# A two-FFN attention block on one core: rows turned on VectorE and by plain transfers, the shift's parts on ScalarE and GpSimd, all of x loaded early

## The chip, the cores and the metric

The kernel runs on one core of one Trainium2 chip. The metric is the device time of one execution, in microseconds. A core has a matrix engine (TensorE; PE in the profile, its weight loads PEld), three engines for elementwise work (VectorE = DVE, ScalarE = ACT, GpSimd = POOL), and queues that issue transfers (SyncE = SP, and the ACT queue).

## The reference, cut to what matters

The input x holds 32 sequences of 256 rows with 128 columns. Every row passes through three residual steps, and the weights of the two FFNs are signs (+1 or -1):

```python
x = x + 0.5 * ffn(layernorm(x))
x = x + attn(layernorm(x))           # attn ends in layernorm(ctx + its input) * gamma + beta
x = x + 0.5 * ffn(layernorm(x))

def ffn(x):                          # 128 -> 512 -> 512 -> 128
    h = concatenate([x, -x])         # (k0 has 256 rows)
    h = relu(s0 * h @ sign(k0)) * 2
    h = relu(s1 * h @ sign(k1)) * 2
    return s2 * h @ sign(k2)

def attn(x):                         # 16 heads of 8 columns, 256 keys
    Q, K, V = x @ Wq.T + bq, x @ Wk.T + bk, x @ Wv.T + bv
    p = softmax(Q @ K.T / sqrt(8))
    return layernorm(p @ V + x) * gamma + beta
```

## The kernel before, in words

**Units.** The work is cut into 16 units of two sequences (512 rows, four tiles of 128). A unit passes through `first` (FFN 0), `norm_attn`, `project`, then for each of its two sequences `maxima`, `shift`, `weigh`, `context`, and at last `second` (FFN 1), which stores the unit. The last unit does FFN 1 in two halves.

**Two halves of a number.** Each fp32 operand of a dense product is split into two fp16 parts, high and low, and both are multiplied. `relu_split` makes them: ACT writes the high part (L625) and DVE the low part (L626); for some tiles ACT writes the whole fp32 value instead (L628, tile `full`) and POOL subtracts (L623).

**Turning.** A dense product needs its rows turned, features on partitions. `normalize` makes the layer-normed rows: `bn_stats` on DVE (L557, L558), the power on POOL (L559, L561), then two POOL passes (L571, L572), or DVE scalings (L566) where `quick` is set. `turned` then turns them. If `quick`, PE transposes them (L585), ACT and DVE split (L588, L589). Else ACT writes the high part (L593), POOL the low part (L594), and one transposing transfer from the SP queue turns both (L595). There are 43 of these transfers: 14 for FFN 0 (`xT`), 15 for attention (`xTa`), 14 for FFN 1 (`xT_None`).

**Attention.** `project` makes Q and K on PE, splits them (L728, L730), writes them to DRAM (L733, tile `dr`) and reads them back into the layout of the score products (L738). The last rows of a Q tile hold the negated row maxima, so that the product subtracts them: the tile is first zeroed by a transfer from a zero block (L717), and the maxima come later. `maxima` makes eight score tiles `nat` per sequence (PE L781) and DVE reduces each to its negated row maxima `nm` (L792). `shift` turns the maxima into the two fp16 parts `mt`: L802 the high part, L803 the low part, both on DVE; PE transposes them (L809, tile `pm`), ACT copies (L814), and two small transfers put them into Q (L815, L816). `weigh` makes the shifted scores `sc` (PE L849), ACT takes the exponential (L861), PE multiplies with V (L831, tile `cx`). `context` transposes back (L875), divides, adds, normalizes and adds to x.

**The order.** It isn't left to the compiler. Each operation is a node with an engine, an estimated cost, a rank and what it reads and writes. `_Plan.simulate` plays the five engines forward with these costs and delays (for a transfer, a `lag` from issue to landing), and picks on each engine the lowest rank that is ready. The instruction order per engine that comes out is written down and fixed; at run time each engine runs its list in order and waits on semaphores. So an estimate that is too low in the list of costs becomes a wait on the chip. A unit of rank (`UNIT`, 16) is one unit of work; the score tiles of one sequence (`nat`) and of the sequence before it (`sc`) are issued as pairs of the same rank and use two PSUM buffers. `choose` orders PE, `relief` decides where L628 takes the place of L626. Constants at the top (`B0`, `BA`, `BP`, `B1`, `AHEAD`, `FAR` and so on) set the ranks of the stages.

The lines that matter below are these:

```python
        op(DVE, 0.2, lambda: nc.vector.tensor_scalar(mt.t[:, :, :, 0, :], nm.t, 1.0 / ONE, ...       # L802
        op(DVE, 0.12, lambda: nc.vector.scalar_tensor_tensor(mt.t[:, :, :, 1, :], nm.t, 1.0 / ONE,   # L803
            mt.t[:, :, :, 0, :], ALU.mult, ALU.subtract), r=[*nmr, (mt, 0)], w=[(mt, 1)], rank=rank)
        op(PE, 0.12, turn, r=[(mt, 0), (mt, 1), "ident16"], w=[pm], rank=(u + 0.5 * b) * UNIT + 8.06, kind="C")
```

## Time and profile before

| what | value |
|---|---|
| median of 3 runs | 693.76 us (691.03 to 695.23) |
| profiled execution | 695.02 us, of which the span is 693.2 us |
| PE busy | 644.7 us (93%) |
| DVE busy | 600.2 us (87%) |
| ACT busy | 536.6 us (77%) |
| POOL busy | 458.8 us (66%) |
| transfers | 46.69 MB, mean 67 GB/s |
| granted PE clock, mean | 0.990 |

The span runs from the first to the last instruction; the 1.8 us around it belong to the execution's own time. Busy time is a union: matmuls on different 32-column tiles of the array overlap and count once. A line such as `L809 <- DVE mt L803` names an instruction that waited and the instruction that released it.

### The profile page before, as it was taken

How to read it: one execution, taken by the hardware profiler on the slowest of the kernel's cores; microseconds unless marked ns; L12 is line 12 of the kernel's file. 1: busy time of each engine (PE TensorE's matmuls, PEld its weight loads, DVE VectorE, ACT ScalarE, POOL GpSimd, SP SyncE). 2: the span in 40 equal slices, each digit the busy share in tenths (PEclk: the TensorE clock that was granted, in tenths of full speed). 3: DMA queues.
4: the chain of work that ended last, by engine and by line, in shares of the span. 5: the costliest groups of instructions: out<-in, count | busy, mean ns of one | idle time of the engine just before them, and what ended most of it. 6: DMA issues, size and time to landing. Idle time of an engine off the chain costs nothing.

```text
span 693.2 us, 29847 instructions
## 1 busy us (share of the span) xinstructions
PE 644.7 (93%) x13082; PEld 330.4 (48%) x13082; DVE 600.2 (87%) x1227; ACT 536.6 (77%) x792; POOL 458.8 (66%) x585
## 2 busy tenths in 40 slices
PE   3989879899999999999999999999999998988997
PEld 1544434545455454545445454544545453543445
DVE  6879988889989888999988898999989888888675
ACT  3545867888889787988888788887878887877773
POOL 6766677679595958869594978866474967653110
PEclk9999979999999999999999999999999999999999
DMA  5142342323333141313323143322213151302000
GB/s 155 45 110 64 73 126 19 103 50 97 56 64 98 26 133 35 111 44 72 94 42 113 34 112 43 70 71 59 75 20 117 22 115 24 88 26 35 5 17 31
DMA packets 79398, 46.69 MB, mean 67 GB/s; under 512 B 50562, under 2 KB 74628, under 8 KB 79268
## 3 DMA queue, kind: packets, MB, share of 16 engines
q1 hardware_dynamic: 77380, 43.93, 26.5%
q8 instruction: 102, 1.67, 1.0%
q10 hardware_dynamic: 1888, 0.85, 0.5%
q14 instruction: 28, 0.23, 0.1%
HBM read 20.25 MB, written 13.24 MB: 48 GB/s over the span
## 4 chain that ended last, share of the span: by engine, by line
PE 70%; DVE 15%; ACT 9%; issue 3%; DMA 2%; SPq 1%; ACTq 0%; POOL 0%
PE p_None L386 17%; PE cx L831 15%; PE p L386 15%; PE sc L849 7%; DVE nm L792 5%; ACT pt L861 5%; PE p L383 4%; PE nat L781 3%; PE p_None L383 2%; PE tp L875 2%; DVE mt L803 2%; PE pv L386 1%; ACT qkhl L728 1%; DVE qkhl L730 1%; PE pq L383 1%
## 5 line engine op out<-in xcount | busy, mean ns | idle before, releaser
L792 DVE TENSOR_REDUCE nm<-nat 128x4 f32<-128x1024 f32 x256 | 310.8, 1217 | 35.7 <-PE nat L781 31.5
L861 ACT ACTIVATE pt<-sc,esc 128x1024 f32<-128x1024 f32 x256 | 285.7, 1118 | 71.4 <-PE nat L781 59.2
L386 PEld LDWEIGHTS <-w 128*32 128x32 f16 x4048 | 103.5, 96 | 97.6 <-issue 31.0
L831 PE MATMUL cx<-pt,vaug 128*32 128x256 f32 x2048 | 139.0, 389 | 0.0
L849 PE MATMUL sc<-Q,ks 32*128 32x256 f16 x1024 | 105.1, 275 | 12.6 <-ACT pt L861 12.2
L781 PE MATMUL nat<-ks,Q 32*128 32x256 f16 x1024 | 102.0, 274 | 2.6 <-ACT pt L861 1.3
L386 PE MATMUL p<-h1h,w 128*32 128x512 f16 x860 | 87.0, 383 | 0.1
L386 PE MATMUL p<-h1l,w 128*32 128x512 f16 x860 | 86.3, 380 | 0.0
L386 PE MATMUL p_None<-h1h_None,w 128*32 128x512 f16 x800 | 80.6, 382 | 0.9 <-ACT full L628 0.8
L831 PEld LDWEIGHTS cx<-pt,vaug 128*32 128x32 f32 x2048 | 59.0, 110 | 47.0 <-issue 16.7
L386 PE MATMUL p_None<-h1l_None,w 128*32 128x512 f16 x800 | 80.4, 379 | 0.3 <-issue 0.3
L849 PEld LDWEIGHTS <-ks 32*128 32x128 f16 x1024 | 32.9, 92 | 71.4 <-issue 65.8
L625 ACT ACTIVATE h2h<-p 128x512 f16<-128x512 f32 (+1 forms) x72 | 41.1, 572 | 22.1 <-PE p L383 11.8
L625 ACT ACTIVATE h1h<-p 128x512 f16<-128x512 f32 (+1 forms) x72 | 40.3, 575 | 14.8 <-PE p L383 10.5
L781 PEld LDWEIGHTS <-Q 32*128 32x128 f16 x1024 | 32.1, 92 | 39.1 <-issue 38.3
L626 DVE SCALAR_TENSOR_TENSOR h2l<-p,h2h 128x512 f16<-128x512 f32 (+1 forms) x63 | 41.0, 651 | 10.5 <-ACT h2h L625 10.3
L559 POOL TENSOR_SCALAR ve_a<-mv_a 128x4 f32<-128x4 f32 (+1 forms) x17 | 3.3, 194 | 69.0 <-PE sc L849 40.5
L383 PEld LDWEIGHTS <-w 128*128 128x128 f16 x308 | 29.6, 100 | 29.4 <-issue 10.5
L626 DVE SCALAR_TENSOR_TENSOR h1l<-p,h1h 128x512 f16<-128x512 f32 (+1 forms) x59 | 38.1, 655 | 4.5 <-ACT h1h L625 4.2
L625 ACT ACTIVATE h2h_None<-p_None 128x512 f16<-128x512 f32 x60 | 35.7, 595 | 6.9 <-PE p_None L386 4.2
L625 ACT ACTIVATE h1h_None<-p_None 128x512 f16<-128x512 f32 x60 | 34.5, 605 | 5.4 <-PE p_None L386 5.3
L386 PE MATMUL p_None<-xT_None,w 128*32 128x512 f16 x480 | 36.6, 390 | 0.9 <-issue 0.6
(159 smaller groups left out, 1376.5 us busy)
## 6 DMA issues: line engine op xcount, KB each, us to landing
dr<-qkhl SPq DMA_DIRECT2D x32, 256.0 KB
Q<-dr SPq DMA_DIRECT2D x48, 128.0 KB
ks<-dr SPq DMA_DIRECT2D x48, 128.0 KB
out_dram<-x SPq DMA_DIRECT2D x15, 256.0 KB
x<-in_L_attn_x_dram SPq DMA_DIRECT2D x14, 256.0 KB
Q<-nought SPq DMA_DIRECT2D x16, 128.0 KB
dm<-mr SPq DMA_DIRECT2D x32, 16.0 KB
Q<-dm SPq DMA_DIRECT2D x32, 16.0 KB
```

Of the source, the lines that this page charges most:

```text
L383: nc.tensor.matmul(to, w, of, start=start, stop=stop)
L386: nc.tensor.matmul(to[32 * r : 32 * r + 32], w[:, 32 * r : 32 * r + 32], of, start=start, stop=stop)
L625: op(ACT, 0.09 + w / 1280, lambda: nc.scalar.activation(hi.t[:, m, :], ps.t, AF.Relu), r=[ps], w=[(hi, m)], rank=rank)
L626: op(DVE, 0.08 + w / 985, lambda: nc.vector.scalar_tensor_tensor(lo.t[:, m, :], ps.t, 0.0, hi.t[:, m, :], ALU.max, ALU.subtract), r=[ps, ( ...
L728: op(ACT, 0.586, lambda i=i, pq=pq, hl=hl: nc.scalar.activation(hl.t[:, 0, :], pq.t, AF.Identity, bias=bs[:, i : i + 1]), r=[pq, "bs"], w= ...
L781: nc.tensor.matmul(nat.t[:, ii, qc, :], Q.t[32 * r : 32 * r + 32, g, b * S + qc * P : b * S + qc * P + P], K[32 * r : 32 * r + 32, g, b * ...
L792: op(DVE, 1.141, lambda g=g, pr=pr, nat=nat: nc.vector.tensor_reduce(nm.t[:, :, 2 * pr : 2 * pr + 2, g].rearrange("p q i -> p i q"), nat.t ...
L803: op(DVE, 0.12, lambda: nc.vector.scalar_tensor_tensor(mt.t[:, :, :, 1, :], nm.t, 1.0 / ONE, mt.t[:, :, :, 0, :], ALU.mult, ALU.subtract), ...
L831: nc.tensor.matmul(cx.t[32 * r : 32 * r + 32, g // 2, :], V[:, 2 * b + kc, 4 * (g // 2) + r, 16 * (g % 2) : 16 * (g % 2) + 32], pts[g, r / ...
L849: nc.tensor.matmul(sc.t[:, ii, kc, :], K[32 * r : 32 * r + 32, g, b * S + kc * P : b * S + kc * P + P], Q.t[32 * r : 32 * r + 32, g, b * S ...
L861: op(ACT, 1.012, lambda pt=pt, sc=sc: nc.scalar.activation(pt.t, sc.t, AF.Exp, scale=esc), r=[sc, "esc"], w=[pt], rank=rank - RUSH, rush=True)
L875: nc.tensor.transpose(tp.t[:, qc, 8 * c : 8 * c + 8, :].rearrange("p h n -> p (h n)"), cxT.t[:, c, bass.ts(qc, P)], ident)
```

## The change

Five things are changed together, and the ranks are set anew.

1. **Turning.** Rows that are not `quick` are turned as fp32: DVE transposes 32x32 blocks (one instruction for a unit), one plain transfer writes 256 KB to DRAM, four plain transfers of 64 KB read it back with the blocks exchanged, and only then ACT writes the high part and POOL the low part. There are 42 of these chains, and no transposing transfer is left. The two attention norms of the first two units are `quick` (one before).
2. **Shift.** The high part of the maxima is written by ACT, a scaled copy and the low part by POOL; DVE does neither.
3. **x and Q.** All units of x are loaded at the start of the SP queue. Q lives in three fixed tiles, zeroed once by POOL; a later unit zeroes only the 8 rows that the shift uses (32 KB in place of 128 KB).
4. **relu.** A new rule `divert` lets ACT write only the whole fp32 value and POOL make both halves: a cast and a subtraction.
5. **Opening.** PE runs 24 products of the identity at the start. Unit 0's norm stands ahead of the weights' preparation, the large POOL memsets wait for it, k0 is asked for earlier, two of four slices of w1 go to POOL, and two small bias transfers and their POOL copies go away.

```diff
+    if WARM:
+        warm = psum([P, P], "warm")
+        def spin():
+            for _ in range(WARM):
+                nc.tensor.matmul(warm.t, ident, ident, start=True, stop=True)
+        op(PE, 0.22 * WARM, spin, r=["ident"], w=[warm], rank=-960)
...
-            hl = buf(work, [P, 2, n, D], F16, "hl", NHL, f"hl{name}")
-            op(ACT, 0.52, lambda: nc.scalar.copy(hl.t[:, 0], xn.t), r=xns, w=[(hl, 0)], rank=rank)
-            op(POOL, 1.12, lambda: nc.gpsimd.tensor_tensor(hl.t[:, 1], xn.t, hl.t[:, 0], ALU.subtract), r=[*xns, (hl, 0)], w=[(hl, 1)], rank=rank)
-            op(SP, 1.35, lambda: nc.sync.dma_start_transpose(
-                out=xT.t.rearrange("p a (t q) -> p (a t) q", q=P), in_=hl.t.rearrange("p a t d -> p (a t d)")),
-               r=[(hl, 0), (hl, 1)], w=[(xT, i, a) for i in range(2) for a in range(0, n, 2)], rank=rank, lag=3.5)
+            tb = buf(work, [P, 4, n, 32], F32, "tb", NTB, f"tb{name}")
+            tf = buf(work, [P, 4, n, 32], F32, "tf", NTF, f"tf{name}")
+            td = buf(dram, [P, 4, n * 32], F32, "td", 4, f"td{name}")
+            op(DVE, 0.06 + n * 0.135, lambda: nc.vector.transpose(tb.t.rearrange("p j t b -> p t j b"), xn.t.rearrange("p t (j a) -> p t j a", a=32)),
+               r=xns, w=[tb], rank=rank)
+            op(SP, 0.53, lambda: nc.sync.dma_start(out=td.t, in_=tb.t.rearrange("p j t b -> p j (t b)")), r=[tb], w=[td], rank=rank, lag=1.8)
+            for j in range(4):
+                op(SP, 0.5, lambda j=j: nc.sync.dma_start(out=tf.t[32 * j : 32 * j + 32].rearrange("a i t b -> a i (t b)"),
+                                                          in_=td.t[:, j, :].rearrange("(i a) n -> a i n", i=4)),
+                   r=[td], w=[(tf, j)], rank=rank, lag=2.0)
+            tfs = [(tf, j) for j in range(4)]
+            order = lambda k: xT.t[:, k].rearrange("p (t i b) -> p i t b", i=4, b=32)
+            parts = lambda k: [(xT, k, a) for a in range(0, n, 2)]
+            op(ACT, 0.12 + 0.1 * n, lambda: nc.scalar.copy(order(0), tf.t), r=tfs, w=parts(0), rank=rank)
+            op(POOL, 0.1 + 0.255 * n, lambda: nc.gpsimd.tensor_tensor(order(1), tf.t, order(0), ALU.subtract), r=[*tfs, *parts(0)], w=parts(1), rank=rank)
...
-        e, eng, rank = (ACT, nc.scalar, -898) if u == 1 else (SP, nc.sync, (u - 2) * UNIT + B0)
+        e, eng, rank = (ACT, nc.scalar, -898) if u == 1 else (SP, nc.sync, u - (690 if u > 3 else 710))
...
-        xTs[key] = turned(xn, key[0][-1], name, n, rank, quick)
+        xTs[key] = turned(xn, key[0][-1], name, n, rank + LATE, quick)
...
+        h.pair = (l, lambda: nc.scalar.activation(full.t, ps.t, AF.Relu), full, CAST * w / 512, lambda: nc.gpsimd.tensor_copy(hi.t[:, m, :], full.t),
+                  0.1 + w / 500, low(full))
...
-        Q = buf(work, [P, G, TU], F16, "Q", 3, f"Q_{u}")
-        qs[u] = Q
-        op(SP, 0.5, lambda: nc.sync.dma_start(out=Q.t.rearrange("(x j) g n -> j x g n", j=4)[3], in_=nought), ...
+        Q = qs[j]
+        if u >= NV:
+            op(SP, 0.4, lambda: nc.sync.dma_start(out=Q.rearrange("(x j) g n -> j x g n", j=16)[3], in_=nought), ...
...
-        op(DVE, 0.2, lambda: nc.vector.tensor_scalar(mt.t[:, :, :, 0, :], nm.t, 1.0 / ONE, None, ALU.mult), r=nmr, w=[(mt, 0)], rank=rank)
-        op(DVE, 0.12, lambda: nc.vector.scalar_tensor_tensor(mt.t[:, :, :, 1, :], nm.t, 1.0 / ONE, mt.t[:, :, :, 0, :], ALU.mult, ALU.subtract),
-           r=[*nmr, (mt, 0)], w=[(mt, 1)], rank=rank)
+        op(ACT, 0.2, lambda: nc.scalar.mul(mt.t[:, :, :, 0, :], nm.t, 1.0 / ONE), r=nmr, w=[(mt, 0)], rank=rank)
+        op(POOL, 0.25, lambda: nc.gpsimd.tensor_scalar(ns.t, nm.t, 1.0 / ONE, None, ALU.mult), r=nmr, w=[ns], rank=rank)
+        op(POOL, 0.3, lambda: nc.gpsimd.tensor_tensor(mt.t[:, :, :, 1, :], ns.t, mt.t[:, :, :, 0, :], ALU.subtract), r=[ns, (mt, 0)], w=[(mt, 1)], rank=rank)
```

## The prediction

> **What bounds the kernel now.** I read the page's engine line first, then the table by stage, then the waits of PE, then the timeline around the wait that stood out. Engine line, and two rows of the table by stage (span, busy time of PE, PEld, DVE, ACT, POOL, granted clock, DMA share, GB/s):
>
> ```profile
> PE 644.7 (93%) x13082; PEld 330.4 (48%) x13082; DVE 600.2 (87%) x1227; ACT 536.6 (77%) x792; POOL 458.8 (66%) x585
> ...
> 75.30:126.30 51.00, 42.85 (x771) 20.35 (x775) 43.34 (x85) 38.08 (x50) 36.48 (x46) 0.90 0.31 65
> 126.30:541.40 415.10, 404.87 (x9060) 208.95 (x9056) 374.92 (x736) 347.28 (x507) 301.78 (x376) 1.00 0.30 72
> ```
>
> Between 126 and 541 us PE is busy 97.5%; the chain that ended last shows the same products at 199.20 and 238.33 us, so a unit takes 39.1 us there. What PE lacks is in its waits. Over the whole span:
>
> ```profile
> PEld L809 <- DVE mt L803: 18.3, 25, 1.4
> ...
> PE pm L809 <- DVE mt L803: 8.8, 14, 1.1
> ```
>
> PE's only repeated wait in the steady part is for the low half of the shift, L803. Its own row says why (duration min, median, max):
>
> ```profile
> L803 DVE SCALAR_TENSOR_TENSOR mt<-nm,mt x32: 166/898/1167, 60.6 to 647.1; 128x32 f16<-128x32 f32 x32
> ```
>
> A pass that can take 166 ns takes 898. The timeline of DVE, POOL and PE shows what it waits for:
>
> ```profile
> 205.82 1.00 DVE L803 SCALAR_TENSOR_TENSOR mt<-nm,mt 128x32 f16<-128x32 f32 x1
> 205.49 1.27 POOL L680 TENSOR_TENSOR x<-x,full 128x512 f32<-128x512 f32 x1
> 226.24 0.90 DVE L803 SCALAR_TENSOR_TENSOR mt<-nm,mt 128x32 f16<-128x32 f32 x1
> 225.93 1.16 POOL L623 TENSOR_TENSOR h2l_None<-full,h2h_None 128x512 f16<-128x512 f32 x1
> 205.87 0.28 PE L849 MATMUL sc<-Q,ks 32*128 32x256 f16 x1
> 206.87 0.23 PE L809 MATMUL pm<-ident,mt 128*32 128x128 f16 x1 [0.60 <-DVE mt L803]
> ```
>
> L803 ends at 206.82 and 227.14, the POOL pass under way at 206.76 and 227.09: it ends 0.05 us after it, both times. The kernel's list holds it for 0.12 us, so PE meets `pm` too early.
>
> **The parts, and their sum.** The sum goes against the profiled span of 693.2 us; its execution took 695.02, so 1.8 lie around it, and the median is 1.3 below that execution.
>
> *Shift: the gain.* After a pair of score tiles, PE's next work normally starts 0.33 us after the pair (203.04 to 203.37). At 205.87 it starts at 206.87: 0.67 lost. In the unit's other sequence the pair at 226.23 is followed by two pieces of 0.22 each, so `pm` was due at 226.99 and starts at 227.19: 0.20 lost. Read so at all 32 `pm`, the losses come to 14 us (ten steady units at about 0.9, and single ones of 0.7 to 1.2 at the start and the end). The 8.8 and 18.3 us of the wait rows bound it: 8.8 below, 27 above.
>
> The new chain is ACT's high part, POOL's scaled copy and POOL's difference. ACT: nearest rows L814 (32x256, 352 ns) and L404 (128x128, 0.30). POOL: L538 copies 128x32 in 237 ns; a subtraction of 128x256 takes 613. So 0.55 us at best, and at worst behind one exponential (1.12) and one 1.04 pass that the order puts between POOL's two: 3.1. The old chain took 1.6 (reduction ends 205.22, L803 206.82). The new order also gives more cover: from the last score pair to `pm` PE has one `cx` piece (1.00), 24 `pq` (1.29, the row of 24 such matmuls), a score pair (0.33) and three quarters of layer 2 (1.34), 3.96 in all, against 2.83 before (203.37 to 206.20). In the other sequence the cover grows by 0.4. With POOL's 0.24 + 1.04 + 0.3 = 1.6, as long as the old chain but with 1.1 and 0.4 more cover, the wait falls to nothing or to a tenth each: 3 us left of 14. I take -11, with 0 and -14 as ends, and the worst chain as a rival.
>
> *Turning: off the path if it lands in time.* DVE gains 42 block transposes. The trace has none; the nearest rows are a reduction of 1024 elements in 1217 ns, thus 0.6 for 512, and the 128x256 addition L895 at 510, thus 1.0. At 0.6 it is +25 us; the shift's two passes (0.270 + 0.665, 32 times) give back 30, 23 fewer L626 some 15, 11 more L678 cost 8. DVE's load falls by about 12, and PE covers it: 375 of 415 us before. ACT writes the high part as before, 0.62; it gains the shift's 10 us and loses 8 of L679. POOL gains about 43 us (20 more subtractions at 1.16, 20 casts at about 1, 32 times 0.5 for the shift; 11 fewer L680 at 1.27) and reaches 72%. SP issues 210 transfers for 43; at 0.5 to 0.6 each against 1.27 this is some 60 us more on a queue that mostly sleeps.
>
> The length of the chain counts. A plain 256 KB write landed 2.0 us after its issue at 211.51, and 3.3 when a transposing transfer was ahead (204.21). The reads: four issues at 0.6, and the last lands 2.3 to 3.2 us after it is issued (the `ks` reads at 216.18 and 45.34). Then ACT 0.62 and POOL 1.16: 2.0 + 1.8 + 2.3 + 1.8 = 7.9 us at best, 10.0 at worst. In the changed order PE has some 9.7 us of work between the transpose of FFN 1's rows and their first product, and 19 to 29 us for the other two kinds. So two chains in three are covered; FFN 1's is covered by -0.3 to +1.8. What is late there first is ACT's copy, and behind it in ACT's list stands the next exponential. I take +2 for 14 such chains, ends 0 and +15.
>
> The Trainium skill speaks against this part: "DMA: Bandwidth & Descriptors", section "Rules for kernel authors", wants turns done by the transposing transfer, since a plain copy with a rearranged pattern is put at 19 times its cost. In the trace a transposing transfer needed 2.5 us from issue to its last packet (202.88 to 205.4); by that factor each turn would need an estimated 47 us, and every unit would stand still for tens of microseconds. I go by the rows, because DVE exchanges the single elements and the transfers move runs of 512 B, and this trace has plain transfers of such runs at ordinary times.
>
> *Opening: -3.5.* The chain that ended last has, in the first layer:
>
> ```profile
> 13.30 2.29 PE p L383 x5
> ...
> 15.80 5.23 PE p L383 x18
> ...
> 24.03 0.97 PE p L383 x4
> ```
>
> That is 458, 290 and 243 ns each, and 216 from 18.5 on: PE starts at half clock. Twenty-three matmuls lose 5 x 242 + 18 x 74 ns = 2.5 us. The 24 spin products start when the identity is there, at about 1.4 us. The `cx` rows price an fp32 product of 256 columns at 0.43 us, thus 0.22 for 128, twice that at half clock. So the spin ends between 6.6 and 11.8 us and the clock is up for the first layer. The norm itself waited: L559 of unit 0 began at 5.83 behind three memsets although its statistics were there at 4.7, and the scalings L566 took 0.7 a pair (1.37 and 1.41 us rows, other work between) behind further memsets. Freed, the first product could start near 10.5 in place of 13.30. Both together give at most 5.5; since the spin may end late and x of unit 1, which DVE now needs before unit 0 is through, shares the queue with more loads, I take 3.5, ends 0 and 6.
>
> "TensorE: Matmul & The Clock Gate", section "What's actually happening", puts full clock after one busy window of about 3.4 us; here it came about 7 us after the first PE work at 11.2. By the page the spin would end near an estimated 9 us, by the trace's 7 us near 10.
>
> *The rest: 0.* Loading x at once adds 3 MB to the opening's transfers, hidden behind 40 us in which only unit 0's and 1's rows are needed. The smaller zeroing saves 1.6 MB that nothing waited for. PE has the same products, 536 changes of tile shape against 546. The end (from 626 us, PE 56.6 busy of 66.9) keeps its order; I allow 4 us either way for it and for the start of the pipeline.
>
> Sum: 693.2 - 11 + 2 - 3.5 = 680.7, with 1.8 around it 682.5 where the profiled execution has 695.02; against the median that is 681.
>
> **The rivals.** *A new wait eats the gain (685 to 700).* FFN 1's chain at its worst costs 1.1 us for 14 units, 15 us; with the shift's gain of 11 and the opening the time is 693.8 - 11 - 3.5 + 15 = 694. For: ACT and POOL run their lists in order, and 9.7 us of cover is no more than the chain. Against: before, transfers nearly as long are met by PE without a wait.
>
> *DVE becomes the bound.* Before, 375 us of DVE in 10.6 units are 35.3 a unit of 39.1; at 0.6 a transpose it becomes about 34.6 of 38.2, at 1.0 it is 35.6. Only from 2.0 us each would DVE set the pace; at 1.5 its queueing already costs PE a few tenths a pair, and the time stays near 688.
>
> *The slower side: the shift waits behind long POOL passes.* The difference now stands in POOL's list, where the passes are of 1.04 to 1.27 us, and its high half behind ACT's exponential. At the worst chain of 3.1 us, 1.5 more than the old one, the added cover of 1.1 and 0.4 is passed by 0.4 and 1.1, so PE loses 0.75 more than before at each of 32 shifts: 693.8 + 24 - 3.5 = 714. It is slower by 1% from a chain of about 2.7 us, against the 1.6 that I take. Against: POOL has 28% idle.
>
> *It does nothing:* if L803 was late only because PE was early anyway, and the next wait stands right behind, only the opening remains: 690.
>
> **How the numbers follow.** The forecast, 0.62, with its own range of 674 to 688. A new wait eats the gain 0.18, DVE 0.04, nothing 0.03, slower side 0.13. The range reaches from a full 14 + 6 with a little at the end, 670, to the upper end of the new wait and part of the slower side, 700. One per cent, about what a measurement can tell from no change here, is 6.9 us: below 686.9 lies nearly all of the forecast and some of the second case, 0.68; 0.18 within; 0.14 above 700.7.
>
> **What would show it.** Right: no wait of PE on `mt`, or a tenth each; units at 38.0 to 38.3 us in the steady part; the first layer at 216 ns a matmul, first score tile near 46 us (49.3 before). Wrong: ACT idle before the copy of FFN 1's rows for a transfer, PE waiting on `pm` for POOL, block transposes above 1.5 us, or units still near 39.

## The result and the profile after

The changed kernel is slower: a median of 711.81 us (710.64 to 714.74, four runs) against 692.39 us for the kernel before (690.72 to 695.23, four runs on the same chip). The ratio is 1.0282, with an interval of 1.023 to 1.0335. The forecast was 681, in a range of 670 to 700. The profiled execution has a span of 711.2 us against 693.2.

The engine line of the page says little: PE, DVE and ACT are busy for nearly as long as before, and POOL for 41 us more.

```profile
PE 653.0 (92%) x12862; PEld 336.0 (47%) x12862; DVE 605.4 (85%) x1199; ACT 533.1 (75%) x817; POOL 499.7 (70%) x681
```

The table by stage says where the 18.0 us are. I cut both kernels at the same events: the first score tile of unit 0, of unit 2's second sequence, and of unit 13's second sequence. The columns are the stretch, its length, busy time of PE, PEld, DVE, ACT, POOL, granted clock, DMA share and GB/s. The kernel after:

```profile
0.00:58.00 58.00, 45.23 (x260) 26.11 (x264) 40.83 (x119) 23.65 (x51) 34.90 (x56) 0.88 0.41 125
58.00:137.20 79.20, 66.04 (x1331) 31.64 (x1332) 68.64 (x125) 54.62 (x82) 58.09 (x76) 0.98 0.24 74
137.20:571.20 434.00, 422.66 (x9151) 215.08 (x9148) 392.59 (x751) 356.86 (x537) 344.11 (x456) 1.00 0.26 83
571.20:711.20 140.00, 119.07 (x2138) 63.15 (x2134) 103.34 (x206) 98.01 (x148) 62.58 (x96) 0.98 0.14 45
```

The kernel before, cut at the same events:

```profile
0.00:49.30 49.30, 36.19 (x208) 17.89 (x212) 36.29 (x124) 23.47 (x48) 33.32 (x55) 1.00 0.41 108
49.30:126.30 77.00, 67.91 (x1306) 31.70 (x1310) 68.49 (x127) 54.71 (x78) 54.14 (x63) 0.93 0.30 68
126.30:560.50 434.20, 423.97 (x9469) 218.72 (x9469) 390.27 (x760) 362.36 (x527) 317.31 (x394) 1.00 0.30 70
560.50:693.20 132.70, 116.64 (x2119) 62.07 (x2115) 105.16 (x219) 96.06 (x141) 53.99 (x75) 0.99 0.16 43
```

So the opening lost 8.7 us, the start of the pipeline 2.2, the end 7.3, and the eleven steady units, where most of the 11 us were to be gained, moved by 0.2. Yet the wait that was to go did go. These are rows of the waits after (engine, line, what was waited for: total, times, longest):

```profile
PEld L874 <- POOL mt L869: 4.7, 6, 1.2
PE pm L874 <- POOL mt L869: 2.8, 4, 1.0
PE pv L423 <- issue: 4.1, 4, 1.4
PE p L423 <- issue: 2.1, 2, 1.2
ACT xT_None L653 <- DMA tf_None<-td_None: 6.4, 4, 2.6
```

PE now waits at `pm` four times where it waited 14 times, and the pass that makes the low half has one duration, where the old one ranged up to 1167 ns (the row of L869: minimum, median, maximum):

```profile
L869 POOL TENSOR_TENSOR mt<-ns,mt x32: 247/252/258, 69.1 to 663.1; 128x32 f16<-128x32 f32 x32
```

Counted by one rule, from the score pair to `pm`, the losses at the 32 `pm` fell from 15.8 to 8.0 us, and in a steady unit from 1.02 to 0.18. (The prediction's reading gave 14 for the 15.8; this count leaves some 0.08 at a `pm` that meets no wait. PE's plain idle time in the same stretches fell from 9.6 to 3.8.) What took the place of the wait shows in the other rows of that fence. "issue" is time in which the engine waited for nothing that the profile shows. The timeline of PE has it a few microseconds behind a `pm` that met no wait:

```profile
456.14 0.22 PE L874 MATMUL pm<-ident,mt 128*32 128x128 f16 x1
...
457.24 0.85 PE L423 MATMUL pv<-wqkv,xTa 128*32 128x128 f16 x48
457.90 0.40 PE L423 MATMUL p<-xT,w 128*32 128x512 f16 x4
459.54 0.40 PE L423 MATMUL p<-xT,w 128*32 128x512 f16 x4 [1.23 <-issue]
```

PE stands still for 1.23 us in the middle of a group of equal products, with no semaphore to wait for. This happens six times after, 0.89 to 1.37 us each and 7.1 in all (6.2 of them in the steady part), and twice before, 1.6 in all. The place gives the cause away. Counted over PE's weight loads and products and the few dozen semaphore and drain instructions among them, the first instruction behind each stop is number 194 of a block of 256, in both kernels and in every experiment below that has a stop. Each time a packet of 16 KB in the DMA queue of kind "instruction" had landed 1.4 to 1.5 us before PE went on (1.1 to 1.6 over all runs). The queue's row, after (packets, MB, share):

```profile
q8 instruction: 100, 1.64, 1.0%
```

PE has 25,782 such instructions. Without the first 193 they make 99.96 blocks of 256. The kernel before has 26,228, thus 101.7 blocks, and 102 such packets; rounded up, the count gives the number of packets in every run below. So PE's program arrives in blocks of 256 instructions, and PE stops where it has run through a block before the next one is there. At the stops of all these traces the 256 before had gone by in 2.1 to 3.6 us of running; some blocks as fast don't stop, so the time alone decides nothing (256 in 2.3 us at 496 us in the kernel after). The small products on quarters of the array go by so fast (`pv`: 96 instructions in 0.67 us). The changed order sets `pv` and the quartered layer 2 close together, and the wait at `pm` no longer stands between them.

### The profile page after: what moved, and what is told of

Read it like the earlier page. It is cut to its first block, busy times and chain, and to the rows that moved or that the text cites. A ratio compares the mean times of both kernels' runs of the same rounds, so it can differ in the third digit from the quotient of the medians.

```text
span 711.2 us, 29766 instructions
## 1 busy us (share of the span) xinstructions
PE 653.0 (92%) x12862; PEld 336.0 (47%) x12862; DVE 605.4 (85%) x1199; ACT 533.1 (75%) x817; POOL 499.7 (70%) x681
## 4 chain that ended last, share of the span: by engine, by line
PE 54%; DVE 19%; DMA 9%; ACT 6%; POOL 5%; issue 3%; SPq 3%; ACTq 0%; DVEq 0%; POOLq 0%
PE p_None L423 13%; PE p L423 11%; PE cx L896 11%; DVE nm L855 9%; PE sc L914 5%; PE p L420 5%; PE p_None L420 3%; DMA tf_None<-td_None 3%; ACT pt L926 2%; PE nat L844 2%; DVE h1l_None L683 2%; SPq L647 2%; PE tp L940 1%; DMA x<-in_L_attn_x_dram 1%; DMA dr<-qkhl 1%
## 5 line engine op out<-in xcount | busy, mean ns | idle before, releaser
L914 PE MATMUL sc<-qs,ks 32*128 32x256 f16 x1024 | 106.7, 274 | 17.9 <-ACT pt L926 17.2
L844 PE MATMUL nat<-ks,qs 32*128 32x256 f16 x1024 | 101.4, 274 | 9.6 <-DVE nm L855 2.7
L423 PE MATMUL p<-h1h,w 128*32 128x512 f16 x716 | 70.8, 384 | 0.2 <-DVE qkhl L793 0.2
L423 PE MATMUL p<-h1l,w 128*32 128x512 f16 x716 | 70.5, 382 | 0.0
L844 PEld LDWEIGHTS <-qs 32*128 32x128 f16 x1024 | 32.1, 92 | 44.7 <-issue 44.2
L420 PEld LDWEIGHTS <-w 128*128 128x128 f16 x342 | 33.3, 101 | 35.6 <-issue 14.9
L683 DVE SCALAR_TENSOR_TENSOR h2l_None<-p_None,h2h_None 128x512 f16<-128x512 f32 x51 | 35.1, 688 | 16.2 <-ACT h2h_None L682 15.9
L680 POOL TENSOR_TENSOR h2l<-full,h2h 128x512 f16<-128x512 f32 (+1 forms) x32 | 36.3, 1134 | 7.6 <-ACT full L685 7.4
L680 POOL TENSOR_TENSOR h1l<-full,h1h 128x512 f16<-128x512 f32 (+1 forms) x31 | 34.0, 1098 | 9.8 <-ACT full L685 9.5
L420 PE MATMUL p<-h1h,w 128*128 128x512 f16 (+1 forms) x109 | 38.5, 365 | 1.3 <-DVE h1l L683 0.5
L420 PE MATMUL p<-h1l,w 128*128 128x512 f16 (+1 forms) x109 | 38.2, 363 | 0.0
```

Source lines behind the costliest of these rows:

```text
L420: nc.tensor.matmul(to, w, of, start=start, stop=stop)
L423: nc.tensor.matmul(to[32 * r : 32 * r + 32], w[:, 32 * r : 32 * r + 32], of, start=start, stop=stop)
L680: return lambda: nc.gpsimd.tensor_tensor(lo.t[:, m, :], of.t, hi.t[:, m, :], ALU.subtract)
L683: l = op(DVE, 0.08 + w / 985, lambda: nc.vector.scalar_tensor_tensor(lo.t[:, m, :], ps.t, 0.0, hi.t[:, m, :], ALU.max, ALU.subtract), r=[p ...
L844: nc.tensor.matmul(nat.t[:, ii, qc, :], Q[32 * r : 32 * r + 32, g, b * S + qc * P : b * S + qc * P + P], K[32 * r : 32 * r + 32, g, b * S ...
L914: nc.tensor.matmul(sc.t[:, ii, kc, :], K[32 * r : 32 * r + 32, g, b * S + kc * P : b * S + kc * P + P], Q[32 * r : 32 * r + 32, g, b * S : ...
```

## The experiments

Kernels whose names begin with b are edits of the kernel before, those with a of the kernel after. In all of them the planner's order is kept, and only what is named is changed. The table is in microseconds: the median of the runs, its ratio to the kernel before on the same chip with the interval (over the chips that kernel's median goes from 690.3 to 693.4, so small differences of medians are to be read by the ratios), and from the profiled run the first score tile, the steady part, the end (both cut as above) and PE's stops for its program.

| kernel | median | ratio, interval | first tile | steady | end | stops |
|---|---|---|---|---|---|---|
| before | 692.39 | | 49.3 | 434.2 | 132.7 | 1.6 |
| after | 711.81 | 1.0282, 1.023–1.0335 | 58.0 | 434.0 | 140.0 | 7.1 |
| b_shift | 704.34 | 1.0192, 1.0171–1.0213 | 48.3 | 443.3 | 134.3 | 2.6 |
| a_shift_back | 713.28 | 1.0326, 1.0308–1.0344 | 55.4 | 435.7 | 140.6 | 1.0 |
| a_memsets | 702.09 | 1.0163, 1.0117–1.021 | 53.0 | 434.3 | 137.9 | 7.4 |
| a_xlater | 705.59 | 1.0214, 1.0187–1.0241 | 55.6 | 432.9 | 138.2 | 5.2 |
| a_nospin | 704.10 | 1.0165, 1.0138–1.0193 | 57.0 | 429.9 | 138.1 | 4.6 |
| a_pvD | 699.84 | 1.0098, 1.0066–1.0129 | 57.8 | 427.2 | 137.3 | 2.0 |
| a_pvD_shift_back | 711.22 | 1.0257, 1.0213–1.03 | 57.5 | 433.4 | 139.6 | 0.7 |
| b_pm32 | 705.46 | 1.0191, 1.0166–1.0216 | 47.4 | 440.4 | 140.9 | 0.7 |
| b_pm32_pvD | 705.88 | 1.0186, 1.0164–1.0207 | 48.1 | 441.7 | 140.3 | 3.4 |
| a_turn_list | 727.11 | 1.0478, 1.044–1.0517 | 57.1 | 449.3 | 136.0 | 3.0 |
| a_mem_x_pvD | 695.47 | 1.0033, 1.0009–1.0058 | 50.0 | 426.2 | 136.8 | 2.9 |
| a_mem_x_pvD_l2D | 692.78 | 0.999, 0.9968–1.0012 | 50.9 | 425.7 | 135.8 | 0 |
| a_end | 712.44 | 1.0275, 1.0242–1.0308 | 57.9 | 435.8 | 138.8 | 8.1 |
| a_best | 692.40 | 0.9991, 0.9976–1.0007 | 50.0 | 425.6 | 137.0 | 0 |
| a_best2 | 698.72 | 1.0088, 1.006–1.0116 | 56.1 | 425.7 | 135.6 | 0 |

### b_shift: the engine switch alone

```diff
-        nc.vector.tensor_scalar(mt.t[:, :, :, 0, :], nm.t, 1.0 / ONE, None, ALU.mult)
-        nc.vector.scalar_tensor_tensor(mt.t[:, :, :, 1, :], nm.t, 1.0 / ONE, mt.t[:, :, :, 0, :], ALU.mult, ALU.subtract)
+        nc.scalar.mul(mt.t[:, :, :, 0, :], nm.t, 1.0 / ONE)
+        nc.gpsimd.tensor_scalar(ns.t, nm.t, 1.0 / ONE, None, ALU.mult)
+        nc.gpsimd.tensor_tensor(mt.t[:, :, :, 1, :], ns.t, mt.t[:, :, :, 0, :], ALU.subtract)
```

> The kernel before with its written-down order kept, and only the shift's parts changed: ACT writes the high part, POOL the scaled copy and the low part, each at the place where DVE had them. Theory: the shift's gain is real and stands by itself. PE's losses at pm (some 0.7 us in one sequence of a unit and 0.2 in the other) fall to a tenth each, L803's 0.9 us pass is gone, and the time falls by 8 to 12 us, to 681 to 685. Rival: the next wait stands right behind this one; the losses at pm vanish but PE waits elsewhere, and the time stays at 689 to 693.

It is 14 us slower than the kernel before, and neither side had that. The losses at `pm` rose to 27.3 us. The timeline shows the slower rival of the prediction at work, a long POOL pass ahead of the short one:

```profile
206.13 1.26 POOL L680 TENSOR_TENSOR x<-x,full 128x512 f32<-128x512 f32 x1
207.35 0.25 POOL L809 TENSOR_TENSOR mt<-ns,mt 128x32 f16<-128x32 f32 x1
207.66 0.23 PE L814 MATMUL pm<-ident,mt 128*32 128x128 f16 x1 [1.31 <-POOL mt L809]
```

The scaled copy had ended at 206.05. The difference then stood behind 1.26 us of other work. So the engine switch by itself lengthens the wait in the old order. The next run shows that the new order by itself doesn't remove it either. The two belong together: the new order puts more PE work ahead of `pm` and mostly keeps long passes out of POOL's list there.

### a_shift_back: the switch undone in the new order

```diff
-        nc.scalar.mul(mt.t[:, :, :, 0, :], nm.t, 1.0 / ONE)
-        nc.gpsimd.tensor_scalar(ns.t, nm.t, 1.0 / ONE, None, ALU.mult)
-        nc.gpsimd.tensor_tensor(mt.t[:, :, :, 1, :], ns.t, mt.t[:, :, :, 0, :], ALU.subtract)
+        nc.vector.tensor_scalar(mt.t[:, :, :, 0, :], nm.t, 1.0 / ONE, None, ALU.mult)
+        nc.vector.scalar_tensor_tensor(mt.t[:, :, :, 1, :], nm.t, 1.0 / ONE, mt.t[:, :, :, 0, :], ALU.mult, ALU.subtract)
```

> The changed kernel with its order kept, and only the shift's parts put back on DVE, at the places where ACT and POOL had them. Theory: the shift's gain is inside the 711 us and was paid away elsewhere, so taking it back costs what was forecast: low parts of about 0.9 us, PE's waits on mt return, 719 to 724 us. Rival: the changed order has enough cover before pm that it is indifferent who makes the parts: 709 to 713 us and no more than 0.1 us lost at each pm.

The wait came back and the time hardly followed it: 713.28 against 711.81, and the intervals of the two ratios overlap. Two rows of its waits:

```profile
PEld L874 <- DVE mt L869: 19.9, 18, 2.5
PE pm L874 <- DVE mt L869: 15.0, 16, 2.2
```

The losses at `pm` are 24.4 us, 16 more than after, and PE's stops for its program fell from 7.1 to 1.0. In the steady part alone PE now idles 8.7 us at `pm` in place of none, and 0.6 at stops in place of 6.2; the part is 1.7 us longer. A PE that waits at `pm` gives the next block time to arrive. There one wait stood in for another, and that suggested the next experiment. The losses at the start and the end aren't followed here; the opening was 2.6 us shorter, within the spread shown below.

### a_pvD: fewer instructions for the same products

`pv` runs on the whole array, in 24 instructions a unit in place of 96.

```diff
-  dense(pv.t[:, t, :], xT.t[:, b, bass.ts(t, P)], wqkv[:, 2, a, :], tiling, k == 0, k == 2)
+  dense(pv.t[:, t, :], xT.t[:, b, bass.ts(t, P)], wqkv[:, 2, a, :], "D", k == 0, k == 2)
```

> The changed kernel with its order kept; only the value products pv are issued as 12 products of the whole array in place of 48 of a quarter each, 24 instructions in place of 96 in each unit, for the same 0.67 us. Theory: PE's stalls without a semaphore (7.1 us in six places) come from 256 instructions going by faster than the next 16 KB of program arrive, so with 72 fewer in the densest stretch they shrink to under 3 us; two more changes of the tile shape a unit cost up to 3 us; time 706 to 710. Rival: the stalls don't hang on the number of instructions; they stay at about 7 us and the time rises by the changes of shape, to 713 to 716.

It is 12 us faster than after, more than was expected. Two stops are left, 0.64 us at the start of the end part and 1.35 in the steady part:

```profile
488.72 0.27 PE L914 MATMUL sc<-qs,ks 32*128 32x256 f16 x1 [1.35 <-issue]
```

The steady part fell by 6.8 us, where the stops fell by 4.9 (6.2 to 1.35):

```profile
134.80:562.00 427.20, 422.08 (x8757) 213.95 (x8748) 392.82 (x751) 356.97 (x537) 344.31 (x456) 1.00 0.26 84
```

The other 1.9 there aren't assigned. The rest of the 12 lies at the start and the end, where it isn't separated from the spread between runs of one opening (below).

### a_pvD_shift_back: the switch undone where the program is no limit

The edits of a_pvD and a_shift_back together.

> The changed kernel with its order kept, the value products issued as 24 instructions a unit in place of 96 (as in a_pvD, 699.8 us), and the shift's parts back on DVE (as in a_shift_back). Theory: in the changed kernel the wait at pm and the wait for the next 16 KB of program stand in the same 4 us of a unit, so that one takes the place of the other and a_shift_back cost only 1.5 us. With the program's wait gone, the shift's gain must show: 708 to 712 us, some 10 above a_pvD, and about 1.2 us lost again at one pm in each unit. Rival: PE is held to the same pace by something else in that stretch; within 3 us of a_pvD.

It takes 711.22 against 699.84: 11.4 us lost by putting the shift's two passes back on DVE (6.2 of them in the steady part), where the same edit cost 1.5 with quartered `pv`. Its row of the waits, beside stops of only 0.7:

```profile
PE pm L874 <- DVE mt L869: 15.7, 16, 2.2
```

So in the new order the switch is worth some 11 us once PE's program is out of the way. That this is the prediction's own number is partly luck. The passes stand here at places that were not made for them, and PE idles 17.8 us ahead of the `pm`, not the 9.6 of the kernel before.

### a_memsets: the nine large memsets moved on POOL

```diff
+        after(pows[0], blank[0])
+        after(next(t for t in pows if t[1] == "a"), blank[1] + take(("ones", 1)))
+        after([g[0].tag for g in order if g[0].tag and g[0].tag[0] == "mult"][1], blank[2] + take(("ones", 2)))
```

Each set of three moves to another place of POOL's list: the first behind the powers of unit 0's norm, the second behind those of the first attention norm, the third behind a later norm.

> The changed kernel with its order kept, but POOL's nine large memsets moved: those of the first tile set into the time in which POOL idles (6.6 to 12.4 us), the others behind 37 us. Theory: the opening lost its time because DVE's scalings L612 of unit 1 (5.65 us for four that need 1.0) and L543 (2.45 us against 0.2) stood still beside POOL's memsets. Then L612 ends near 19 us in place of 22.1, L543 takes 1.2 us or less, the first score tile starts at 53 to 55 us in place of 58.0, and the time is 706 to 709. Rival: the opening is late because of x and PE's order; first score tile at 57 to 58 and 710 to 712 us.

The theory of the opening holds: the first score tile comes at 53.0 in place of 58.0. The kernel takes 702.09 (two runs, 704.39 and 699.79), faster than was expected; what the start and the end gave isn't explained. Behind this stands a lock between DVE and POOL. In the kernel after, DVE's four scalings of unit 1 lie beside an unbroken row of POOL work, and one instruction on 3x3 elements beside another row, which lasts from 31.77 to 34.14 (timeline of DVE, POOL and PE):

```profile
16.43 5.75 DVE L612 TENSOR_SCALAR fxn<-x,mv_f,rs_f 128x128 f32<-128x128 f32 x4
31.71 2.45 DVE L543 TENSOR_SCALAR diag<-ident,top 3x3 f32<-3x3 f32 x1
...
16.67 2.26 POOL L680 TENSOR_TENSOR h1l<-full,h1h 128x512 f16<-128x512 f32 x2 [0.30 <-ACT full L685]
18.87 1.39 POOL L576 MEMSET vaug<- 128x1536 f32 x1
20.19 0.96 POOL L577 MEMSET ks<- 128x1024 int32 x1
21.08 0.95 POOL L584 MEMSET qs<- 128x1024 f32 x1
...
22.17 0.69 PE L632 MATMUL t<-ident,fxn 128*128 128x128 f32 x2 [2.65 <-DVE fxn L612]
```

The scalings end at 22.18 and the POOL row at 22.03. With the memsets elsewhere, the same instructions in a_memsets take half of that, and a tenth for the small one:

```profile
17.48 2.85 DVE L630 TENSOR_SCALAR fxn<-x,mv_f,rs_f 128x128 f32<-128x128 f32 x4
...
28.42 0.21 DVE L561 TENSOR_SCALAR diag<-ident,top 3x3 f32<-3x3 f32 x1
```

The two differences, 2.9 and 2.2, come to the 5.0 us by which the first score tile came earlier.

### a_xlater: most of x behind the weights

```diff
+        after("wide", take("x"))
```

Fourteen loads of x move behind the loads of the projections on the SP queue.

> The changed kernel with its order kept, but the 14 loads of x for units 2 to 15 moved behind the loads of the projections on the SP queue (about 21 us in place of 2 and 11 us). Theory: x of unit 1 landed 6.9 us after its issue because the 512 KB of units 2 and 3 went ahead of it, and DVE, which wants it before it goes on with unit 0, waited until 10.35 us. Then it lands near 8 us, the scale inputs with it, the first product starts at 11 us or earlier in place of 12.72, and the first score tile 1 to 2 us earlier than 58.0. Rival: the load is late behind k1 on its own queue; it lands at 10 us as before, nothing in the opening moves, and the time stays at 710 to 713.

705.59 us. Unit 1's rows are there at about 8.5 us in place of 10.35, and the first product starts at 11.91 in place of 12.72. The first score tile moved by 2.4. But five kernels with the same opening had it at 58.0 (after), 57.9 (a_end), 57.8, 57.5 and 55.4 (a_shift_back), largely by how long the first write of Q and K took to land: 2.1 to 4.1 us over these runs, 3.9 in the kernel after. So about 1 us of the opening is the early loads, and up to some 1.8 of the 8.7 may be chance, by an estimate from these landings (3.9 against 2.1).

### a_nospin: without the 24 products at the start

```diff
-            for _ in range(WARM):
+            for _ in range(0):
```

> The changed kernel with its order kept and the 24 spin products at the start left out. Two questions. First, PE stands still six times for 0.9 to 1.4 us without any semaphore, each time just ahead of the 194th of a row of 256 of its weight loads and products (counted from the start); the spin is 96 of these. Theory: every 256 instructions PE needs the next 16 KB of its program, and where 256 go by in under 4 us it waits for them. Then stalls again stand at count 193 of 256, at other places of the work. Rival: the stalls belong to places of the work (the value products and what follows); then they stay there and the count moves by 96. Second, the spin's worth: if it warms the clock for the first layer, the first score tile (55 to 58 us in the runs with the spin) comes 1 to 2 us later; if PE's wait after the spin lets the clock fall again, nothing moves.

704.10 us, 7.7 less than after, and the first score tile not later (57.0). The spin raised the clock too early: 15 of its products went by in the 3.2 us up to 4.6 us, and the other 33 in the 3.9 after that. The table by stage of the kernel after, granted clock in the last column but two:

```profile
4.60:11.40 6.80, 4.40 (x39) 4.13 (x38) 2.51 (x10) 2.27 (x5) 1.71 (x3) 1.00 0.68 193
11.40:18.20 6.80, 5.49 (x14) 1.76 (x14) 6.32 (x21) 4.34 (x8) 5.17 (x8) 0.50 0.79 228
```

The spin was over at 8.5, PE then waited for the first rows, and when the first layer began at 12.72 the clock was back at half: eight products took 3.60 us, 450 ns each, not 216. Most of the 7.7 us lies elsewhere, 4.1 in the steady part. Leaving the spin out takes 96 instructions from PE's program, so that the blocks end at other places of the units. The stops still stand at number 194 of 256, at other work, and come to 4.6. In the steady part PE's idle rows account for the 4.1: stops fell from 6.2 to 4.3, and PE's waits for ACT's exponentials ahead of `sc` from 2.4 to 0.4. Why the second fell isn't shown; the rest of the 7.7 isn't settled.

### b_pm32 and b_pm32_pvD: another way past the wait

The kernel before, with the fp32 maxima transposed by PE and split afterwards, so that PE needn't wait for the split; their transfer to DRAM becomes two. The second also has a_pvD's edit.

```diff
-        nc.vector.tensor_scalar(mt.t[:, :, :, 0, :], nm.t, ...)      # and the low half, then pm <- mt
+        nc.tensor.transpose(pm.t[:, qc, :], nm.t[:, qc].rearrange("p r g -> p (r g)"), ident)
+        nc.scalar.mul(mr.t[:, 0, :], pm.t.rearrange("p q n -> p (q n)"), 1.0 / ONE)
+        nc.vector.scalar_tensor_tensor(mr.t[:, 1, :], pm.t..., 1.0 / ONE, mr.t[:, 0, :], ALU.mult, ALU.subtract)
```

> The kernel before with its order kept; DVE's two passes ahead of pm go away: PE transposes the fp32 maxima themselves, and only behind pm ACT takes the high part and DVE the low part, both out of PSUM. Theory: PE's losses at pm (15.8 us summed over the run) are then nearly gone, and what the changed kernel showed appears here too: some of them come back as stalls for the program. Time 680 to 686. Rival: PE's next wait stands right behind in the same stretch of the unit (layer 2, pm, value products), and the time stays at 687 to 692.

> As the run before, and the value products issued as 24 instructions in place of 96 a unit. Theory: the stalls for the program that b_pm32 may show stay under 2 us, and the time is 2 to 5 us below that of b_pm32. Rival: the changes of tile shape cost as much as the stalls did; within 1.5 us of b_pm32.

The losses at `pm` fell from 15.8 to about 2.5 us and the time rose by 13, more than even the rival had. The steady part is 6 us longer and the end 8. In the steady part PE's idle time fell from 10.2 to 7.6 us: the 6.9 at `pm` went, and 4.3 more stand at other waits. But PE was busy 8.8 us longer (432.8 against 424.0). Its fp32 transposes take 274 ns each, and in the timeline no other product starts beside them, where the fp16 ones share the array with the products around them: a pair holds PE for some 0.32 us, where one took 0.11. So this run shows that most of the wait came back elsewhere, but with PE's added work it is no clean price of the wait. The end wasn't followed. Whole-array `pv` brings nothing here (705.88): the program was no limit (stops of 0.7), and in this order the stops even rose to 3.4, a spread that isn't explained.

### a_turn_list: the turning undone

ACT and POOL split at the places where DVE turned the blocks, and one transposing transfer takes the place of the five plain ones.

```diff
-            nc.vector.transpose(tb.t.rearrange("p j t b -> p t j b"), xn.t.rearrange("p t (j a) -> p t j a", a=32))
+                nc.scalar.copy(hl.t[:, 0], xn.t)
+                nc.gpsimd.tensor_tensor(hl.t[:, 1], xn.t, hl.t[:, 0], ALU.subtract)
...
+                nc.sync.dma_start_transpose(out=xT.t..., in_=hl.t...)
```

> The changed kernel with its order kept and only the turning undone: at the place of DVE's block transpose ACT and POOL write the two halves, and at the place of the first read one transposing transfer turns them; the write, three reads and the later two passes go away. Theory: the five transfers cost PE 4 us or more in the steady part and as much again at the end, because each of the two hops is lengthened by up to 2 us when a 16 KB program fetch sits on one of the 16 transfer engines. The rows are now there some 3 us earlier, ACT's waits for them (6.4 us for FFN 1) go, and the time is 702 to 707. Rival: ACT's and POOL's passes, moved 5 us ahead in their lists, push the exponentials and the shift's parts back by as much as the chain costs; 709 to 716.

727.11 us, the rival's side. It is no clean price of the turning: ACT's early copy now waits for POOL's norm (nine waits of 12.8 us in all), PE waits for POOL's low halves `h1l` and `h2l` (9.8 us in the steady part), and the POOL passes push the shift back, so that 1.37 us a unit are lost up to `pm`. What it shows is that the changed order can't go back to the old turning at these places.

### a_mem_x_pvD and a_mem_x_pvD_l2D: the parts together

The first has the edits of a_memsets, a_xlater and a_pvD. The second also runs layer 2 on the whole array:

```diff
-  dense(po.t[:, t, :], h2[k].t[:, c, bass.ts(t, P)], w2[:, c, :], tiling, ...)
+  dense(po.t[:, t, :], h2[k].t[:, c, bass.ts(t, P)], w2[:, c, :], "D", ...)
```

> The changed kernel with its order kept and three edits together: the large memsets moved (a_memsets), x of units 2 to 15 loaded behind the projections (a_xlater), the value products as 24 instructions (a_pvD). Theory: the three act in different places, and the gains add for the greater part: first score tile at 51 to 54 us, no more than 1 us of stalls for the program, and 688 to 694 us, level with the kernel before. Rival: the gains of single runs were partly luck in how transfers meet; 696 to 700.

> As a_mem_x_pvD, and layer 2 of both FFNs issued as products of the whole array too: 16 instructions in place of 64 a tile of rows where it was quartered. Theory: fewer fetches of the program and none that PE waits for, so the five-transfer chains are lengthened less often; against that each piece of layer 2 beside quartered work pays two changes of the tile shape. Between -3 and +6 us of a_mem_x_pvD. Rival: the changes of shape cost more than 0.1 us each and decide: +8 us or more.

They take 695.47 and 692.78 us. The first keeps three stops, 2.9 us, more than was expected; its profiled run is the fastest of its ten (692.13). The second is level with the kernel before (0.999, interval 0.9968 to 1.0012). It has no stop at all, and the steady part and the queue's row are

```profile
129.20:554.90 425.70, 423.70 (x7190) 212.44 (x7188) 393.06 (x751) 356.17 (x536) 344.44 (x456) 1.00 0.27 84
```

```profile
q8 instruction: 80, 1.31, 0.8%
```

PE's 20,430 instructions are 79.05 blocks without the first 193; there are 80 packets. 256 of them take at least 6.8 us in the steady part. A unit takes 38.7 us, where the prediction had 38.0 to 38.3 and both kernels 39.5. So 8.5 us of the steady gain can be had. In the profiled runs the opening (+1.6), the start (+1.3) and the end (+3.1) give 6.0 of them back, and over all runs the medians are level.

### a_end and a_best: the shift ahead of POOL's long passes at the end

The kernel after has a long POOL pass ahead of the shift's two in unit 13 (POOL and PE in the timeline):

```profile
589.76 1.16 POOL L680 TENSOR_TENSOR h2l_None<-full,h2h_None 128x512 f16<-128x512 f32 x1
591.00 0.30 POOL L868 TENSOR_SCALAR ns<-nm 128x32 f32<-128x32 f32 x1
591.65 0.25 POOL L869 TENSOR_TENSOR mt<-ns,mt 128x32 f16<-128x32 f32 x1
591.95 0.23 PE L874 MATMUL pm<-ident,mt 128*32 128x128 f16 x1 [0.96 <-POOL mt L869]
```

The maxima were ready at 590.12. Both kernels move that pass, and what stands between the two, behind the shift in units 13 and 14, a_end in the kernel after and a_best in a_mem_x_pvD_l2D.

```diff
+        for u in (13, 14):
+            late = [k for k in range(i) if order[k][0].eng == POOL][-1:] + [k for k in range(i + 1, j) if order[k][0].eng == POOL]
+            order[:] = [g for k, g in enumerate(order[: j + 1]) if k not in late] + [order[k] for k in late] + order[j + 1 :]
```

> The changed kernel with its order kept and only this last edit: the shift's POOL passes of units 13 and 14, second sequence, ahead of the subtraction before them. Theory: 1.1 us less lost at each of the two pm, and 2 us less from unit 13's second sequence (571 us) to the end. Rival: the later subtraction is waited for in place of the shift; the stretch keeps its 140 us.

> As a_mem_x_pvD_l2D (692.8 us, level with the kernel before), and in units 13 and 14 the shift's two POOL passes of the second sequence put ahead of the subtraction L680 that stands before them in POOL's list. Theory: what is left against the kernel before stands at the end, and 1.1 us each of it at those two pm, where PE waits for POOL as the slower-side rival had it. These losses go, the stretch from unit 13's second sequence to the end shortens by about 2 us, and the time is 689 to 691, 0.2 to 0.6% under the kernel before. Rival: layer 2 behind waits for the subtraction that is now later by 1.2 us, and nothing is won; 692 to 694.

The loss at those `pm` fell from 1.10 to 0.07 us each, and the times stayed: 712.44 (ratio 1.0275, 1.0242 to 1.0308) and 692.40 (0.9991, 0.9976 to 1.0007). In a_end the end part is 1.2 us shorter (138.8) and the steady part 1.8 longer, with stops of 8.1 in place of 7.1. In a_best the end is 1.3 us longer than in a_mem_x_pvD_l2D. So these two waits are at most a small part of the 7.3 that the end lost.

### a_best2: more memsets in the row

In a_mem_x_pvD_l2D, two sets of memsets are put behind unit 0's first layer, and unit 1's statistics behind unit 0's scalings.

```diff
+        order[at:at] = blank[1] + blank[2]
+        after(scale[0], early)
```

> As a_mem_x_pvD_l2D, with the opening's lists put in a better order once more: the memsets of the second and third tile set stand where POOL idles behind unit 0's first layer (18 to 29 us) and no longer beside unit 0's attention scalings (3.1 us in place of 0.4 in a_best), DVE scales all of unit 0 before it touches unit 1's rows, and five small DVE passes go behind unit 1's turned rows. Theory: the rest of the opening's loss is the same lock and the same order; the first score tile starts at 46 to 48.5 us in place of 50 to 51, and the time is 688 to 691, 0.3 to 0.7% under the kernel before. Rival: the opening now hangs on when x and the small loads land; first score tile at 49.5 or later and 692 to 694.

The theory's time was wrong: 698.72 us (1.0088, 1.006 to 1.0116), first score tile 56.1. But the run measures the lock. DVE, POOL and PE:

```profile
15.11 8.94 DVE L639 TENSOR_SCALAR fxn<-x,mv_f,rs_f 128x128 f32<-128x128 f32 x4
...
15.18 2.27 POOL L707 TENSOR_TENSOR h1l<-full,h1h 128x512 f16<-128x512 f32 x2
...
22.71 0.95 POOL L611 MEMSET qs<- 128x1024 f32 x1
...
23.80 0.90 PE L659 MATMUL t<-ident,fxn 128*128 128x128 f32 x3 [6.92 <-DVE fxn L639]
```

Beside two POOL passes the four scalings take 2.85 us (a_memsets), beside five 5.75 (after), beside eight 8.94: each time until 0.2 to 0.4 us after the unbroken row of POOL ends.

## Why the prediction was wrong, point by point

**Shift, -11.** The local mechanism held: no more than a tenth of a microsecond is left at a steady `pm`, POOL's pass takes 252 ns, and where PE's program is no limit the switch is worth something like the forecast. The steady part without stops is 8.5 us shorter than before (a_mem_x_pvD_l2D), and undoing the switch costs 11.4 (a_pvD_shift_back). The step that failed is the one from the wait to the time. I took the losses at `pm` for a gain without asking what PE would meet next in the same stretch, and gave the case "the next wait stands right behind" 3 in 100. It stood there: stops of 6.2 us in the steady part, against 1.6. As built, undoing the switch cost 1.5 us (3.0 by the ratios, whose intervals overlap). The rival "a new wait eats the gain" came nearest, but it had only FFN 1's chain for the wait, and put its whole at 694. The slower rival was true in the old order (b_shift), and in the new one only at two `pm` of the end; that its 714 lies near the measured 711.81 is luck.

**Turning, +2.** The block transpose took 0.70 us, near my 0.6, and the chain for FFN 1 took 8.0 to 10.9 us, where I had 7.9 to 10.0. The term was still too small, by an estimate. In the steady part the late copies at 141, 338 and 379 us cost about 4 us: PE idles 1.3 us behind the first, and the units of the other two took 39.3 and 40.9 us where a unit without a stop or a late copy took 38.6. By the same reading the start and unit 14 lost some 4 more; no run priced any of it. In the steady part stops (+4.7) and these (+4) make up for what `pm` gained (-9.2), to within 0.3 us of the measured -0.2. The sign that I had named for it, ACT idle before the copy of FFN 1's rows, is there with 6.4 us in four waits, the longest this one (SP, ACT, PE):

```profile
291.77 0.34 SPq L645 DMA_DIRECT2D td_None<-tb_None  x1
293.86 2.18 SPq L647 DMA_DIRECT2D tf_None<-td_None  x4
...
369.65 0.34 SPq L645 DMA_DIRECT2D td_None<-tb_None  x1
373.73 1.73 SPq L647 DMA_DIRECT2D tf_None<-td_None  x4
...
378.70 0.62 ACT L653 CAST xT_None<-tf_None 128x512 f16<-128x512 f32 x1 [2.63 <-DMA tf_None<-td_None]
...
380.38 0.26 PE L914 MATMUL sc<-qs,ks 32*128 32x256 f16 x1 [1.14 <-ACT pt L926]
```

The read starts 2.1 us after the write's issue in the usual case and 4.1 here. In that second case a 16 KB block of PE's program began to land 1.6 us after the write, and eight of the write's 128 packets came 0.7 to 1.5 us behind the others, 3.5 us after the issue. Five more writes into which such a block fell took 2.9 to 3.6 us to their last packet, against mostly 1.66 without. It holds beyond this trace: from 130 us on in the twelve traces with this chain, 34 of the 38 writes in which a block began to land 0.5 to 1.66 us after the issue took over 2.5 us, and 2 of the 256 with no block beside them. Why the packets come late isn't shown, and no run changed this alone.

The rule of "DMA: Bandwidth & Descriptors", section "Rules for kernel authors", by which each turn would have needed an estimated 47 us, is not borne out for these transfers: the whole chain, with its two hops, a copy and a subtraction, took 8.0 to 10.9 for FFN 1 and 8.7 to 14.9 for the other rows. DVE had exchanged the single elements and the transfers moved runs of 512 B, so the plain rearranged copy that the rule speaks of wasn't run.

**Opening, -3.5; it was +8.7.** Two steps failed. The prediction freed the norm from the memsets of unit 0's time and never asked beside what they would stand next. They stood beside DVE's scalings and the 3x3 product: 5.0 us, by a_memsets. It is the same lock that the prediction itself had read off L803, 0.05 us after a POOL pass. The spin's 2.5 us is the second: the spin ended at 8.5 us, earlier than the 9 to 10 that the page's and the trace's waits gave, and the clock fell again before the first layer. (The trace's 7 us was counted from 11.2, but PE's first work before stands at 8.60.) The risk that was named, x of unit 1 landing late, cost about 1 us, and the first product started at 12.72 where I had 10.5. Before it had started at 12.44, not at the 13.30 of the row that I read, which is that of the next five products; so the freed norm brought PE's first layer no earlier.

**The rest, 0 ± 4.** The start lost 2.2 us and the end 7.3, more than I allowed. The end holds unit 14's chain, one stop (0.9) and the two late `pm`; moving the last took 1.2 us off it in a_end and nothing in a_best. PE's waits for ACT's exponentials rose there from 5.9 to 8.5 us. In a_mem_x_pvD_l2D, without stops, 3.1 us of it remain. What these are stays open; no run told it.

**DVE as the bound.** It isn't: it is busy for 392.6 of the 434.0 us of the steady part, against 390.3 of 434.2 before.

## What to carry to other kernels

The sum of a wait bounds what removing it can bring; the gain is known only when the next limit in the same few microseconds is. Put a price on that one before the wait's sum goes into a forecast. When work moves on GpSimd, look at which VectorE passes will stand beside it: here a memset that is free by itself held up a chain until the whole row it stood in was over. And count TensorE's instructions per microsecond as well as its time, since here small tiles outran the arrival of the program.

## What the runs showed of the hardware that was not expected

- PE's program comes in packets of 16 KB, one for 256 instructions, and PE stopped 0.4 to 1.4 us at some of the places where 256 had gone by in 2.1 to 3.6 us. The Trainium skill, "Runtime: NRT & Kernel Launch", section "Instruction fetch mechanics", has the 16 KiB blocks of 256 instructions, and calls their cost mostly hidden. The packets here agree with the size. Of the kernel after's 100 blocks 94 were hidden; the six others cost 7.1 us, as much as half of the wait that the change was to remove.
- DVE's scalings beside POOL ended when the unbroken row of POOL had ended, whether that was two, five or eight instructions (2.85, 5.75, 8.94 us). "SBUF — State Buffer", section "Who interferes with whom", has the loser of the shared port blocked for the other's instruction; here it was blocked for the row.
- The clock came up 3.2 us after the spin's first product, near the 3.4 us that "TensorE: Matmul & The Clock Gate", section "What's actually happening", states, and was lost again at 11.4, after 3.4 us in which PE was busy for 1.0. Here the work that warmed PE up brought nothing, since the real work didn't follow at once.
